# Two banded convolution layers: part of the input statistics summed by ScalarE instead of VectorE

## The chip, the cores and the metric

The kernel runs on one core of one Trainium2 chip. The metric is the device time of one execution in microseconds, the median of several runs. The core has a matrix engine (PE, with its weight loads PEld), VectorE (DVE), ScalarE (ACT), GpSimd (POOL), the queue engine SyncE (SP), and 16 DMA engines. POOL also issues DMAs of its own.

## The reference

The input `x` is 1 x 512 x 512 x 64 in float32. Two layers of one form follow each other, each adding its result to `x`. What matters here is that a layer begins with a group normalization whose 32 groups (two channels each) take mean and variance over the whole 512 x 512 picture, so that no value of a layer can be normalized before all of its input has been read.

```python
def _gn(v, G=32, eps=1e-5):
    g = v.reshape(B_, H_, W_, G, C_ // G)
    m = jnp.mean(g, axis=(1, 2, 4), keepdims=True)
    s = jnp.var(g, axis=(1, 2, 4), keepdims=True)
    return ((g - m) / jnp.sqrt(s + eps)).reshape(v.shape)
x = x + _L0_conv_ref(_gn(x), ...)   # layer norm, gated projections, band product, layer norm, projection
x = x + _L1_conv_ref(_gn(x), ...)
```

## The kernel before

The kernel has three stages. The first (`input_stats`, line 414) reads all of `x` once for the statistics of the first group normalization. The other two (`layer`, run as the generators `one` and `two`) are software pipelines over units of eight columns, with an order written out by hand in the tables `FIRST` and `SECOND`. The statistics of the second normalization are gathered inside the first layer by PE, so only the first stage concerns us.

In the first stage `x` is cut into 16 tiles `gn_x` of 128 partitions x 128 pixels x 64 channels, 4 MB each, in three buffers. SP issues one DMA per tile. For each tile DVE runs 32 `bn_stats`, one per group, each over 128 x 256 numbers, which leave mean and squared deviation of even and odd elements in `gn_st`. Then `gather` (line 432), one to five small POOL instructions (on DVE for the last tile), folds the tile's results into the running sums `gn_s1`, `gn_s2` and `gn_own`. From the third tile on, `meanwhile` lets DVE and PE do one step of `solve_layer` (line 314), the preparation of the two layers' weights. After the last tile DVE and PE reduce the sums over partitions and `group_affine` computes the scale `ga` and the shift `gb`; the first layer's first instruction `z<-z,ga` needs them.

The weights, biases and masks of both layers are fetched by small DMAs which POOL issues (`fetch_layer`, line 281, called at line 1177 before `input_stats`). Most instructions are issued through `en`, whose wrapper `InOrder` pins each of them behind the instruction traced before it on the same engine:

```python
def __getattr__(self, name):                       # class InOrder, line 483
    f = getattr(self.engine, name)
    return lambda *a, **k: tc.keep_in_program_order(f(*a, **k))   # line 491
got = [fetch_layer(i, v, tmp) for i, v in enumerate(layers)]      # line 1177; then input_stats
```

So the profile gives line 491 for most instructions, and they are told apart by their tiles. The first POOL instructions through `en` are the two memsets of `gn_s1` and `gn_s2`. After the stage SP goes on with the loads `z` of the first layer's first units, the zero fill of `left_of` and the load `on<-left_w`, which stand in its queue behind the sixteenth `gn_x`.

Of the kernel before, what the change touches and what calls it, by code (L numbers as in the profile page):

```python
# [10 lines left out]
F32 = mybir.dt.float32  # L11
I32 = mybir.dt.int32
BF16 = mybir.dt.bfloat16
AF = mybir.ActivationFunctionType
# [5 lines left out]
P = 128  # L20
# [8 lines left out]
LAG = 2 * NU  # L29
NZ = 12  # L30
NX = 6
RING = LAG + 2
WIDE = 512
NB = 32
# [97 lines left out]
def last(v: bass.AP, n: int) -> bass.AP:  # L132

    p, c = v.shape
    return v.unsqueeze(2).broadcast_to([p, c, n])
# [22 lines left out]
def tile_two_banded_layers(  # L158
# [10 lines left out]
    G = D // 2  # L169
# [45 lines left out]
    def any_bank():  # L215
        return two_banks(next(turns))[:, :512]
# [175 lines left out]
    def spread(o: bass.AP, v: bass.AP):  # L392

        nc.vector.tensor_copy(o.rearrange("p (g t) -> p g t", t=2), last(v, 2))
# [12 lines left out]
    def group_affine(mean: bass.AP, var: bass.AP, pool):  # L407

        ve = pool.tile([P, D], F32, name="g_ve")
        nc.vector.tensor_scalar(ve, var, GN_EPS, None, ALU.add)  # L410
        rsqrt(ga, ve, pool)
        nc.vector.scalar_tensor_tensor(gb, mean, -1.0, ga, ALU.mult, ALU.mult)

    def input_stats(meanwhile, afterwards):
        flat = x.rearrange("h w c -> (h w) c").rearrange("(p n) c -> p n c", p=P)
        per = L * L // P
        nt = min(128, per)
        n_t = per // nt
        with tc.tile_pool(name="gnx", bufs=3) as gx, tc.tile_pool(name="gns", bufs=1) as gs:
            st = gs.tile([P, G, n_t, 6], F32, name="gn_st")  # L420
            parts = st.rearrange("p g t (s k) -> p g (t s) k", k=3)
            add, sub, mult = ALU.add, ALU.subtract, ALU.mult

            def two(nm: str):
                return gs.tile([P, G, 2], F32, name=nm)

            own, s1, s2 = two("gn_own"), two("gn_s1"), two("gn_s2")
            ref = parts[:, :, 0:2, 1]
            en.gpsimd.memset(s1, 0.0)
            en.gpsimd.memset(s2, 0.0)  # L430

            def gather(t: int, engine):
                if t == 0:
                    engine.tensor_copy(own, parts[:, :, 0:2, 2])
                    return
                off = two(f"gn_off{t % 2}")
                engine.tensor_tensor(off, parts[:, :, 2 * t : 2 * t + 2, 1], ref, sub)
                engine.tensor_tensor(s1, s1, off, add)
                engine.tensor_tensor(off, off, off, mult)
                engine.tensor_tensor(s2, s2, off, add)  # L440
                engine.tensor_tensor(own, own, parts[:, :, 2 * t : 2 * t + 2, 2], add)

            for t in range(n_t):
                xt = gx.tile([P, nt, D], F32, name="gn_x")
                en.sync.dma_start(xt, flat[:, t * nt : (t + 1) * nt, :])
                for g in range(G):
                    en.vector.bn_stats(st[:, g, t, :], xt[:, :, 2 * g : 2 * g + 2])
                gather(t, en.gpsimd if t < n_t - 1 else en.vector)
                meanwhile(t)
            afterwards()  # L450

            mean, var = two("gn_mean"), two("gn_var")
            nc.vector.scalar_tensor_tensor(mean, s1, 1.0 / n_t, ref, mult, add)
            pm = any_bank()[:, :D]
            flat2 = lambda v: v.rearrange("p g s -> p (g s)")
            nc.tensor.matmul(pm, lhsT=all_ones, rhs=flat2(mean), start=True, stop=True)
            nc.vector.tensor_tensor(var, s1, s1, mult)
            nc.vector.scalar_tensor_tensor(var, var, -1.0 / n_t, s2, mult, add)
            nc.vector.scalar_tensor_tensor(var, own, 1.0 / nt, var, mult, add)
            tot = gs.tile([P, G], F32, name="gn_total")  # L460
            nc.vector.tensor_reduce(tot, pm.rearrange("p (g s) -> p g s", s=2), AX.X, add)
            nc.vector.tensor_scalar(tot, tot, 0.5 / P, None, mult)
            nc.vector.tensor_tensor(mean, mean, last(tot, 2), sub)
            nc.vector.tensor_tensor(mean, mean, mean, mult)
            nc.vector.scalar_tensor_tensor(var, var, 1.0 / n_t, mean, mult, add)
            pv = any_bank()[:, :D]
            nc.tensor.matmul(pv, lhsT=all_ones, rhs=flat2(var), start=True, stop=True)
            mc = gs.tile([P, D], F32, name="gn_mc")
            vc = gs.tile([P, D], F32, name="gn_vc")
            spread(mc, tot)  # L470
            vg = gs.tile([P, G], F32, name="gn_vg")
            nc.vector.tensor_reduce(vg, pv.rearrange("p (g s) -> p g s", s=2), AX.X, add)
            nc.vector.tensor_scalar(
                vc.rearrange("p (g t) -> p g t", t=2), last(vg, 2), 0.5 / P, None, mult
            )
            group_affine(mc, vc, gs)
# [105 lines left out]
    def kept(u: Unit):  # L582
        en.scalar.activation(
            ZT[:, u.at % RING].rearrange("c k (n p) -> c n k p", n=2),
            u.pt.rearrange("c n (k p) -> c n k p", p=S), AF.Identity, bias=1.0,
# [10 lines left out]
    def left_kept(u: Unit):  # L596
        pt = one_bank().rearrange("c (k p) -> c k p", p=P)
        for k in range(JU // 2):
            en.tensor.transpose(
                pt[:, k], u.z[:, 2 * k : 2 * k + 2, :].rearrange("p j c -> p (j c)"), ident  # L600
            )
        u.t = ZT[:, u.at % RING]
        en.scalar.activation(u.t, pt, AF.Identity, bias=1.0)
# [5 lines left out]
    def crossed(u: Unit, q: int, w: bass.AP, b: str):  # L609

        u.banks[q], pr = take(b)
        pr = pr.rearrange("p (e k h) -> p e k h", e=2, k=JQ // 2)
        turns = ZT[:, u.at % RING], u.t
        for k in range(JQ // 2):
# [210 lines left out]
    def gates(o: Out, w: dict, b: str):  # L825
# [3 lines left out]
        for e in range(2):  # L829
            part = slice(e * D, (e + 1) * D)  # L830
            en.tensor.matmul(
                o.pg[:, e], lhsT=w["gate"][part],
                rhs=ZT[part, o.at % RING].rearrange("c k (n p) -> c (k n) p", n=2)[:, :, m.lo : m.hi],
                start=True, stop=True,
# [31 lines left out]
    def fetch(src: bass.AP, o: Out, n: int, stats: bool):  # L866
        o.xr = XR[n % NX]
        if stats:
            o.f = o.xr[:, :, 1 : 1 + 2 * D]
        else:  # L870
            o.f = o.xr.rearrange("p k c -> p (k c)")[:, : JU * D].rearrange("p (k c) -> p k c", c=2 * D)
        for e in range(2):
            en.sync.dma_start(o.f[e * S : e * S + o.blk.m], rows_of(src, o, e))
# [41 lines left out]
    def layer(src: bass.AP, dst: bass.AP, w: dict, stats: bool, then=None):  # L915
# [15 lines left out]
        if stats:  # L931
            for n in range(2):
                posts.setdefault(n - 1, []).append(lambda n=n: clear_zh(ZH[n]))
            for n in range(NX):
                posts.setdefault(n, []).append(lambda n=n: clear_xr(XR[n]))
# [235 lines left out]
    with tc.tile_pool(name="setup", bufs=1) as tmp:  # L1171
# [5 lines left out]
        got = [fetch_layer(i, v, tmp) for i, v in enumerate(layers)]  # L1177
# [20 lines left out]
        def meanwhile(t: int):  # L1198

            if t > 1:  # L1200
                next(solving, None)
# [8 lines left out]
        def afterwards():  # L1210
            for _ in solving:
                pass
            next(one)
            for z in left_of.rearrange("a (p m w) -> a p m w", p=P, w=WIDE):
                en.sync.dma_start(z, mid(nothing, z.shape[1]))

        input_stats(meanwhile, afterwards)


# [5 lines left out]
    A = keep.tile([P, H // HA, HA // 2, S, 2], F32, name="A")  # L1225
    ZT = keep.tile([P, RING, JU // 2, P], F32, name="ZT")

# [3 lines left out]

    XR = [keep.tile([P, JU // 2, 2 * D + 2], F32, name=f"XR{i}") for i in range(NX)]
    ZH = [keep.tile([H, 2, JU, S], F32, name=f"ZH{i}") for i in range(2)]

    def clear_xr(t: bass.AP):
        en.vector.memset(t, 0.0)
        for at in (0, 2 * D + 1):
            en.vector.memset(t[:, :, at : at + 1], 1.0)

    def clear_zh(t: bass.AP):  # L1240
        en.scalar.copy(t.rearrange("h n x p -> h (n x p)"), mid(nothing, 2 * JU * S // WIDE))
# [47 lines left out]
```

## Time and profile before

| what | us |
|---|---|
| median of 3 runs | 4260.02 |
| lowest and highest run | 4246.09 and 4260.52 |
| span of the profiled execution | 4279.5 |
| first stage in it, from the start to the first `z<-z,ga` | 212.5 |

The profile gives the profiled execution no time of its own beside its span, which is 19.5 us above the median. A span is read in microseconds from its start. Busy time is the time in which an engine executes; register, semaphore and DMA-issuing instructions don't count as busy. In a timeline each row has a start, a length, the engine, the line, the operation with its tiles, how many instructions were merged into it, and in brackets how long the engine idled before it and what released it. Rows of one engine may overlap a little.

### The profile page before, as it was taken

To read this page: it belongs to the slowest core of one execution; us is meant where nothing else is said; L and a number is where in the kernel's file an instruction comes from. 1 tells how busy PE (TensorE), PEld (TensorE's weight loads), DVE (VectorE), ACT (ScalarE), POOL (GpSimd) and SP (SyncE) were. 2 spreads that over 40 slices of the span, in tenths; PEclk is the share of its full clock that TensorE was granted. 3 is DMA by queue.
4 is the path that set the end of the run, shared out by engine and by line. 5 is a ranking of instruction groups with operands and counts; after the bars stand their busy time and mean duration, and the time that the engine had idled before them with its cause. 6 is when DMAs were issued, how large, how long until landed. Compare 5 with 4: busy or idle time off the path is not lost.

```text
span 4279.5 us, 223070 instructions
## 1 busy us (share of the span) xinstructions
PE 3741.4 (87%) x94986; PEld 3208.3 (75%) x94986; DVE 3681.0 (86%) x9911; ACT 3320.3 (78%) x6372; POOL 3584.7 (84%) x4566
## 2 busy tenths in 40 slices
PE   0158999999999999999975889999999898989998
PEld 0057888888888888888864778787878787878786
DVE  8968888888888888888867889898989898989897
ACT  0047888888888888888863778888889788978887
POOL 2368999999999999999837789898989898989883
PEclk9989999999999999999997999999999999999999
DMA  9843545454545454545344354545454545444533
GB/s 396 321 102 96 150 112 152 117 147 114 152 115 151 116 152 117 153 115 155 104 119 114 98 141 120 145 120 148 121 147 119 146 116 145 123 142 122 149 105 96
DMA packets 695718, 596.25 MB, mean 139 GB/s; under 512 B 138310, under 2 KB 549990, under 8 KB 692420
## 3 DMA queue, kind: packets, MB, share of 16 engines
q1 hardware_dynamic: 692212, 580.43, 47.6%
q8 instruction: 748, 12.26, 1.2%
q14 instruction: 246, 2.02, 0.2%
q0 software_dynamic: 2512, 1.56, 0.1%
HBM read 436.71 MB, written 149.74 MB: 137 GB/s over the span
## 4 chain that ended last, share of the span: by engine, by line
PE 77%; issue 4%; POOL 3%; DVE 3%; SPq 2%; DMA 2%; ACT 2%; POOLq 0%; DVEq 0%; ACTq 0%
PE banks L491 59%; PE bank L491 14%; PE acc L491 4%; POOL z L491 3%; SPq L491 2%; DMA z<-mid_x 1%; POOL on L491 1%; DVE ZH L491 1%; DVE sto L491 1%; DVE RO L491 1%; ACT RO L491 0%; DVE z L491 0%; ACT on L491 0%; DVE XR L491 0%; ACT sg L491 0%
## 5 line engine op out<-in xcount | busy, mean ns | idle before, releaser
L491 ACT ACTIVATE on<-RO,nm,rs 128x128 f32<-128x128 f32 x2484 | 1144.3, 499 | 176.0 <-PE banks L491 150.4
L491 POOL TENSOR_SCALAR on<-RO,rs,nm 128x128 f32<-128x128 f32 x2124 | 958.6, 463 | 354.7 <-PE banks L491 308.4
L491 PE MATMUL banks<-pack,ZT 64*128 64x128 f32 x9216 | 1000.4, 287 | 28.5 <-DVE RO L491 13.9
L491 PE MATMUL banks<-pack,zT 64*128 64x128 f32 x9216 | 947.0, 277 | 3.7 <-issue 3.7
L491 DVE TENSOR_TENSOR RO<-banks,sg 128x512 f32<-128x512 f32 x1152 | 778.3, 684 | 181.9 <-ACT sg L491 158.6
L491 PEld LDWEIGHTS banks<-pack,ZT 64*128 64x128 f32 x9216 | 765.2, 191 | 152.9 <-ACT zT L491 35.6
L491 DVE BATCH_NORM_STATS2 sto<-RO 128x6 f32<-128x256 f32 x2304 | 852.5, 412 | 3.0 <-ACT RO L491 3.0
L491 DVE SCALAR_TENSOR_TENSOR ZH<-banks,pack,ZH 128x896 f32<-128x896 f32 (+1 forms) x576 | 667.4, 1159 | 198.2 <-PE banks L491 153.4
L491 ACT ACTIVATE sg<-banks 128x512 f32<-128x512 f32 x1170 | 691.6, 595 | 171.7 <-PE banks L491 133.0
L491 POOL TENSOR_TENSOR z<-z,ga 128x512 f32<-128x512 f32 x556 | 719.2, 1294 | 111.3 <-DMA z<-mid_x 91.0
L491 PE MATMUL banks<-RO,A 64*64 64x64 f32 x36864 | 699.4, 223 | 122.7 <-issue 117.5
L491 PEld LDWEIGHTS banks<-RO,A 64*64 64x64 f32 x36864 | 623.3, 136 | 222.8 <-issue 160.3
L491 PEld LDWEIGHTS banks<-pack,zT 64*128 64x128 f32 x9216 | 747.9, 192 | 5.0 <-issue 4.1
L491 POOL TENSOR_TENSOR z<-z,gb 128x512 f32<-128x512 f32 x556 | 717.8, 1291 | 3.5
L491 PE MATMUL bank<-pack,ZH 128*64 128x64 f32 x18432 | 666.3, 226 | 21.1 <-DVE ZH L491 11.2
L491 PEld LDWEIGHTS bank<-pack,ZH 128*64 128x64 f32 x18432 | 593.2, 139 | 111.3 <-issue 56.0
L491 ACT COPY RO<-banks 128x1024 f32<-128x1024 f32 x540 | 542.8, 1011 | 163.3 <-PE banks L491 154.1
L491 POOL TENSOR_TENSOR z<-z,rs 128x512 f32<-128x512 f32 x586 | 617.2, 1060 | 50.7 <-DVE rs L491 48.7
L491 POOL TENSOR_TENSOR z<-z,sti 128x512 f32<-128x512 f32 x586 | 621.9, 1071 | 35.8 <-DVE sti L491 31.8
L491 ACT ACTIVATE ZH<-banks 128x896 f32<-128x896 f32 (+1 forms) x576 | 535.4, 929 | 83.1 <-PE bank L491 55.4
L491 PE MATMUL banks<-ZT,pack 64*128 64x448 f32 (+1 forms) x2304 | 573.3, 572 | 2.6 <-DVE ZH L491 1.4
L491 DVE BATCH_NORM_STATS2 sti<-z 128x6 f32<-128x128 f32 x2344 | 509.4, 282 | 63.8 <-POOL z L491 62.9
(202 smaller groups left out, 4053.8 us busy)
## 6 DMA issues: line engine op xcount, KB each, us to landing
z<-in_x_dram SPq DMA_DIRECT2D x576, 128.0 KB
A<-left_of SPq DMA_DIRECT2D x576, 128.0 KB
z<-mid_x SPq DMA_DIRECT2D x576, 128.0 KB
gn_x<-in_x_dram SPq DMA_DIRECT2D x16, 4096.0 KB
XR<-in_x_dram SPq DMA_DIRECT2D x448, 112.0 KB
mid_x<-XR SPq DMA_DIRECT2D x448, 112.0 KB
XR<-mid_x SPq DMA_DIRECT2D x448, 112.0 KB
out_dram<-XR SPq DMA_DIRECT2D x448, 112.0 KB
```

The lines of the kernel that those rows point to most:

```text
L491: return lambda *a, **k: tc.keep_in_program_order(f(*a, **k))
```

## The change

For all tiles but the first, VectorE handles only the groups 0 to 22. The other nine (`GA = 9`, `cut = 23`) are handled by `by_sums`: for each group ScalarE runs two activations over the same 128 x 256 numbers, Identity and Square, each with a bias read from `gn_back` and each summing its output into one number per partition (`accum_out`, tile `gn_got`). The outputs themselves go to a scratch tile `gn_aside`, of which there are two, one for even and one for odd tiles; all 18 activations of a tile write the same one. Six POOL instructions then turn the 18 sums into the form in which `bn_stats` leaves mean and squared deviation, and write it to `gn_st`. The bias `gn_back` is minus the mean of the first tile, one POOL instruction behind the first tile's `bn_stats`.

```diff
--- before.py
+++ after.py
@@ -29,6 +29,7 @@
 LAG = 2 * NU
 NZ = 12
 NX = 6
+GA = 9
 RING = LAG + 2
 WIDE = 512
 NB = 32
@@ -426,6 +427,8 @@
 
             own, s1, s2 = two("gn_own"), two("gn_s1"), two("gn_s2")
             ref = parts[:, :, 0:2, 1]
+            cut = G - GA
+            back = gs.tile([P, GA], F32, name="gn_back")
             en.gpsimd.memset(s1, 0.0)
             en.gpsimd.memset(s2, 0.0)
 
@@ -440,11 +443,36 @@
                 engine.tensor_tensor(s2, s2, off, add)
                 engine.tensor_tensor(own, own, parts[:, :, 2 * t : 2 * t + 2, 2], add)
 
+            def by_sums(t: int, xt: bass.AP):
+
+                aside = gs.tile([P, nt, 2], F32, tag=f"gn_aside{t % 2}", name="gn_aside")
+                got = gs.tile([P, 2, GA], F32, tag=f"gn_got{t % 3}", name="gn_got")
+                for g in range(GA):
+                    c = slice(2 * (cut + g), 2 * (cut + g) + 2)
+                    for n, f in enumerate((AF.Identity, AF.Square)):
+                        en.scalar.activation(
+                            aside, xt[:, :, c], f, bias=back[:, g : g + 1],
+                            accum_out=got[:, n, g : g + 1],
+                        )
+                off, sq = got[:, 0], got[:, 1]
+                side = gs.tile([P, 2, GA], F32, tag=f"gn_side{t % 2}", name="gn_side")
+                en.gpsimd.tensor_scalar(side[:, 0], off, 0.5 / nt, None, mult)
+                en.gpsimd.tensor_tensor(side[:, 1], side[:, 0], off, mult)
+                en.gpsimd.tensor_tensor(side[:, 1], sq, side[:, 1], sub)
+                en.gpsimd.tensor_tensor(side[:, 0], side[:, 0], back, sub)
+                to = parts[:, cut:, 2 * t : 2 * t + 2]
+                en.gpsimd.tensor_scalar(to[:, :, :, 1], last(side[:, 0], 2), 1.0, None, mult)
+                en.gpsimd.tensor_scalar(to[:, :, :, 2], last(side[:, 1], 2), 0.5, None, mult)
+
             for t in range(n_t):
                 xt = gx.tile([P, nt, D], F32, name="gn_x")
                 en.sync.dma_start(xt, flat[:, t * nt : (t + 1) * nt, :])
-                for g in range(G):
+                for g in range(cut if t else G):
                     en.vector.bn_stats(st[:, g, t, :], xt[:, :, 2 * g : 2 * g + 2])
+                if t == 0:
+                    en.gpsimd.tensor_scalar(back, ref[:, cut:, 0], -1.0, None, mult)
+                else:
+                    by_sums(t, xt)
                 gather(t, en.gpsimd if t < n_t - 1 else en.vector)
                 meanwhile(t)
             afterwards()
```

## Rows read from the trace of the kernel before

**Rows 1.** The page, part 1: busy time, share of the span, instructions.

```profile
span 4279.5 us, 223070 instructions
PE 3741.4 (87%) x94986; PEld 3208.3 (75%) x94986; DVE 3681.0 (86%) x9911; ACT 3320.3 (78%) x6372; POOL 3584.7 (84%) x4566
```

**Rows 2.** Busy time by window: PE, PEld, DVE, ACT, POOL, clock, DMA share, GB/s.

```profile
0.00:50.00 50.00, 0.00 (x0) 0.00 (x0) 32.86 (x106) 1.28 (x1) 14.97 (x34) 1.00 0.97 397
...
150.00:200.00 50.00, 3.88 (x8) 1.92 (x8) 48.89 (x163) 0.00 (x0) 9.59 (x25) 1.00 0.90 318
```

**Rows 3.** Timeline of VectorE in the first stage.

```profile
14.12 20.97 DVE L491 BATCH_NORM_STATS2 gn_st<-gn_x 128x6 f32<-128x256 f32 x64 [10.87 <-DMA gn_x<-in_x_dram]
35.61 10.54 DVE L491 BATCH_NORM_STATS2 gn_st<-gn_x 128x6 f32<-128x256 f32 x32 [0.52 <-DMA gn_x<-in_x_dram]
...
193.96 10.53 DVE L491 BATCH_NORM_STATS2 gn_st<-gn_x 128x6 f32<-128x256 f32 x32
204.59 0.27 DVE L491 TENSOR_TENSOR gn_off<-gn_st 128x64 f32<-128x64 f32 x1
...
212.52 1.72 DVE L491 TENSOR_TENSOR z<-z,ga 128x512 f32<-128x512 f32 x1
```

**Rows 4.** Timeline of SP's DMA issues in the first stage.

```profile
0.74 165.65 SPq L491 DMA_DIRECT2D gn_x<-in_x_dram  x16
166.44 26.21 SPq L491 DMA_DIRECT2D z<-in_x_dram  x30
```

**Rows 5.** Timeline of POOL from the start to its first statistics.

```profile
8.66 0.52 POOL L294 DMA_DIRECT2D raw<-in_L_conv_Wrg_dram  x1 [2.57 <-DMA raw<-in_L_conv_Wr_dram]
...
45.85 0.58 POOL L305 DMA_DIRECT2D mq<-in_L_conv_src_mask_dram  x1 [1.04 <-DMA brow<-in_L_conv_bl_dram]
...
47.97 0.55 POOL L294 DMA_DIRECT2D raw<-in_L_conv_Wr_dram  x1 [1.41 <-DMA brow<-in_L_conv_blg_dram]
...
122.22 0.50 POOL L311 DMA_DIRECT2D ci<-in_L_conv_src_mask_dram  x1 [2.42 <-DMA ci<-in_L_conv_src_mask_dram]
122.71 0.25 POOL L491 MEMSET gn_s<- 128x64 f32 x2
122.89 0.30 POOL L491 COPY gn_own<-gn_st 128x64 f32<-128x64 f32 x1
```

**Rows 6.** DMA issues up to 220 us: count, KB each, median us to landing.

```profile
spare<-later_pack POOLq DMA_DIRECT2D x1, 498.5 KB, 4.0
...
brow<-in_L_conv_br_dram POOLq DMA_DIRECT2D x2, 0.5 KB, 18.2
```

**Rows 7.** ScalarE's groups by shape, whole span: busy us, mean ns, idle before.

```profile
L491 ACT ACTIVATE on<-RO,nm,rs 128x128 f32<-128x128 f32 x2484 | 1144.3, 499 | 176.0 <-PE banks L491 150.4 <-POOL on L491 19.4 <-POOL z L491 3.0
L491 ACT ACTIVATE sg<-banks 128x512 f32<-128x512 f32 x1170 | 691.6, 595 | 171.7 <-PE banks L491 133.0 <-DVE RO L491 9.4 <-DVE A L491 2.3
L491 ACT COPY RO<-banks 128x1024 f32<-128x1024 f32 x540 | 542.8, 1011 | 163.3 <-PE banks L491 154.1
...
L491 ACT COPY acc<-sto 128x32 f32<-128x32 f32 x72 | 13.9, 192 | 2.0 <-DVE sto L491 2.0
```

**Rows 8.** Timeline of VectorE, two memsets that write one tile.

```profile
1.17 0.17 DVE L1174 MEMSET half<- 128x128 f32 x1
1.41 0.28 DVE L1176 MEMSET half<- 64x64 f32 x2
```

**Rows 9.** Timeline of ScalarE inside the first layer.

```profile
386.22 0.20 ACT L491 COPY acc<-sto 128x32 f32<-128x32 f32 x1
386.45 0.22 ACT L491 ACTIVATE acc<-sto 128x32 f32<-128x32 f32 x1
386.60 0.58 ACT L491 ACTIVATE ZT<-banks 128x512 f32<-128x512 f32 x1
387.08 0.59 ACT L491 ACTIVATE zT<-banks 128x512 f32<-128x512 f32 x1
```

**Rows 10.** POOL's groups by shape, 0 to 215 us: busy us, mean ns, idle before.

```profile
L491 POOL TENSOR_TENSOR gn_s<-gn_s,gn_off 128x64 f32<-128x64 f32 x28 | 9.0, 320 | 2.1
```

## The prediction

> **What bounds the kernel now.** I first read the page's busy times [rows 1]: VectorE, ScalarE and POOL are all busy for about four fifths of the span, so no engine total decides, and the change has to be judged in the one stage that it touches. That stage runs from 0 to 212.5 us, where the first `z<-z,ga` waits for the statistics [rows 3]; it is 5% of the span. The windows [rows 2] show three things there. ScalarE does nothing but one table load. VectorE is near full from about 14 us on (48.89 of 50 us late in the stage). And the DMA engines were at 0.97 with 397 GB/s at the start. A 4 MB tile (4.194 million bytes) at 397 GB/s takes 10.56 us, and its 32 `bn_stats` take 10.53 us [rows 3]: DMA and VectorE are level. VectorE falls behind only by the weight preparation between the tiles and by the 14.1 us before the first tile has landed. The timeline of VectorE shows tile after tile to 204.5 us, then 7.9 us of small instructions to `ga` (204.59 to 212.52). SP's sixteenth `gn_x` goes out at about 166 us, when VectorE has released a buffer [rows 4].
>
> The view that decides the case is POOL's own timeline [rows 5]. POOL issues the small weight DMAs and may start each only when one issued eight earlier has landed (8.66 us: 2.57 us idle until `raw` had landed); with the `gn_x` stream beside them such a DMA lands after some 18 us [rows 6]. So POOL is still issuing at 122.22 us. The two memsets of `gn_s1` and `gn_s2` need no input at all, yet they run at 122.71, right behind the last of these DMAs: they are pinned behind them. Before the change nothing waits for POOL, which catches up on its small sums from 122.9 us on.
>
> **The change part by part.** *Removed:* nine of 32 `bn_stats` in 15 tiles, 135 of them. At 10.53/32 = 0.329 us each that is 44.4 us of VectorE [rows 3]. Were nothing else added, VectorE would need 7.6 us for a tile plus some 0.6 for preparation, below the DMA's 10.56, so the DMA would set the pace.
>
> *Added wait, and when ScalarE starts.* Every activation of `by_sums` reads `gn_back`. That is a POOL instruction issued through the same wrapper, behind the two memsets, hence behind all weight DMAs [rows 5]. Its data is there at 24.6 us; its turn in the queue is not. What is queued behind it: ScalarE has nothing else, but a tile's buffer is released only when ScalarE has read it. Tile 0 needs no ScalarE, so tile 3 still loads, landing at about 14.1 + 3 x 10.7 = 46 us (10.7 is the step between the first and the third tile). Then three buffers hold tiles 1 to 3, SP's `gn_x` 4 waits, and the stream stops. From here on POOL's DMAs have the DMA engines for themselves. At 46.4 us 44 issues are left before the memsets (47.97 to 122.22 us), 23.7 us of issue time by their rows. Do they still wait for landings? Away from the full stream, 498.5 KB landed in 4.0 us [rows 6], and eight issues of 0.54 us cover 4.3 us, so hardly. I add 2 us for what is in flight at 46 us and 0.7 for memsets and `gn_back`: 46.4 + 23.7 + 2.7 = 72.8, and ScalarE starts at **73 us**. Bounds: 69 without waits and with a few issues earlier, 123 as before if nothing gets faster. I take the value near the lower end because the stream that made the landings slow is certainly absent.
>
> That step leans on one DMA delaying another. The Trainium skill's opening page "Trainium Kernel Development and Optimization" (Key Constraints) says that DMAs issued from SP, ACT and POOL run on the same 16 DMA engines and interleave; the 18 us landing beside the full stream agrees with it [rows 6]. If the queues were separate instead, POOL would be no earlier than 123 us, which is the third rival below.
>
> *One accumulating pass.* The trace has none, so it is built from neighbours [rows 7]. A 128x512 pass without a bias from memory takes 595 ns, a 128x1024 copy 1011 ns: 0.81 ns per element, so 256 elements take 387 ns. A 128x128 `on`, with a scale and a bias from memory, takes 499 ns where the same line gives 283: 108 ns for each such operand. With one bias: 495 ns. Normally successive passes overlap by 0.10 us (`ZT` at 386.60 for 0.58 us, the next at 387.08 [rows 9]). Here all 18 write the same `gn_aside`, and the trace shows what a second write to one tile does: the second memset of `half` starts 0.07 us after the first ended [rows 8] where neighbours overlap, and ScalarE's two writes to `acc`, 386.22 for 0.20 us then 386.45, have a gap of 0.03 us. So I take 495 + 30 = 525 ns without overlap. The sum must also be read out to `gn_got`; no row shows that. It costs between nothing and a smallest copy with its gap, 0.22 us [rows 7, 9]. It moves one number per partition, so I take under half, 0.085. One pass: **0.61 us**; bounds 0.39 (overlap, free readout) and 0.75. A tile is then 18 x 0.61 = 11.0 us, 15 tiles 165 us.
>
> The Trainium skill's page "ScalarE: Activation LUTs" (What ACT_TABLE_LOAD costs) gives a pass with one such operand as about 280 ns + 0.833 ns per element, 493 ns here, and says that back-to-back passes overlap by about 93 ns. Its duration agrees with the 495 worked out from the rows; its overlap would make the pass 0.40 us and belongs to the first rival.
>
> *Sum of the stage.* ScalarE at 11.0 us per tile is slower than the DMA at 10.56, and once started has three tiles ready, so it never waits: 73 + 165 = 238 us. Check: `gn_x` 4 goes out at 84 us and lands by 98, ScalarE wants it at 106. VectorE at 8.2 us per tile is ahead, and POOL with six and five instructions of some 0.35 us has 4 us of work per tile. All that is covered by ScalarE. Behind the last tile come six dependent POOL instructions, 320 ns and a gap of 0.06 each by the nearest row [rows 10], 2.3 us, and a hand-over of 0.1, which used to be hidden because VectorE finished alone. Then the same 7.9 us to `ga`. The first `z<-z,ga` comes at 238 + 2.4 + 7.9 = 248.3 instead of 212.5: **+36 us**. SP's later loads move too: its last `gn_x` goes out when tile 12 is read, at 73 + 132 = 205 us, 43 us ahead of `ga` where it was 46 [rows 3, 4], so the `z` loads stay hidden. If that cover were gone, their 26 us of issue would be the price. The first layer needs `ga`, so the shift passes on whole, and its work is unchanged. No second table load is charged; one would be 1.28 us [rows 2]. The sum in the profile: 4279.5 + 36 = 4315; against the median of the runs, 19.5 us lower, 4260 + 36 = **4296 us**.
>
> **The rivals.** *DMA sets the pace after the late start.* If a pass costs under 0.55 us, ScalarE is the faster one and waits. Then `gn_x` 4 goes out at 73 + 18c (c the pass), is in use 13.4 us later as tile 0 was, tile 15 follows 11 x 10.56 us behind, and ScalarE ends 18c after that: 202.6 + 36c in all, which passes 73 + 270c at c = 0.554. With c = 0.525 that is 221.5 and with c = 0.39 it is 216.6, plus 10.3 to `ga`: +19 and +14 us, 4279 and 4274. Against it stands the shared scratch tile.
>
> *ScalarE starts in time, faster.* If `gn_back` were put ahead of the weight DMAs, ScalarE would start at about 25 us, end at 190 and `ga` would come at 200: -12 us, 4248; with c = 0.5 the DMA would set the pace and end by some 183, -19 us, 4241. The point at which it decides is a start at 37 us with c = 0.61. The memsets at 122.71 speak against it: they had every freedom and stayed behind the DMAs.
>
> *POOL isn't relieved.* If the weight DMAs keep their pace, ScalarE starts at 123 us, and everything comes 50 us later still: +86 us, 4346. Half of the relief gives 98 us and +61, 4321. For it: each of POOL's DMAs has many small pieces, and no row shows them alone.
>
> **How the numbers follow.** About 0.5%, 21 us, is what a measurement of this kernel can tell from no change. My forecast has 0.58, with its own range of 4285 to 4315 (a pass of 0.57 to 0.68). The DMA-paced rival has 0.20, the unrelieved POOL 0.15, the start in time 0.07. The range has to reach the DMA-paced end, less a few us for an earlier start and the runs' spread, and half way into the unrelieved one: 4272 to 4330. Faster by over 0.5% needs an early start and cheap passes together, and a little more than they give: 0.03. Within 0.5% are the other early starts and the DMA-paced cases, which end at +14 to +20 us, less those where POOL is also a little late: 0.22. Slower has the rest, 0.75.
>
> **What would show it.** ScalarE's first pass near 73 us, right behind a POOL instruction `gn_back` that follows the last `ci` DMA; a stop in SP's `gn_x` issues between about 25 and 84 us and a hole in the DMA rate; POOL's issues in close order after 46 us; passes 0.61 us apart without idle time between tiles; VectorE idle in the middle of the stage, waiting for `gn_x`; `z<-z,ga` near 248 us. The prediction is wrong if `gn_back` runs early, if ScalarE's passes come in under 0.5 us, or if the first layer takes up part of the shift.

## The result and the profile after

The changed kernel takes 4298.35 us (median of 5 runs, 4290.62 to 4302.86), the kernel before 4259.38 (median of 5, 4246.09 to 4260.52): a ratio of 1.0091 [1.0075, 1.0106]. That is 39.0 us slower, where +36 was predicted. The profiled execution after has a span of 4292.3 us and took 4294.12.

The page, part 1, of the kernel after (it answers to [rows 1]):

```profile
span 4292.3 us, 223599 instructions
PE 3740.1 (87%) x94986; PEld 3205.7 (75%) x94986; DVE 3636.3 (85%) x9776; ACT 3479.1 (81%) x6912; POOL 3596.4 (84%) x4657
```

The totals did what the change says, and tell nothing of the time: VectorE fell by 44.7 us (3681.0 to 3636.3), ScalarE rose by 158.8 (3320.3 to 3479.1). The windows of the kernel after (start and end, length, then PE, PEld, DVE, ACT, POOL, clock, DMA share, GB/s; they answer to [rows 2]) show where it went:

```profile
25.00:50.00 25.00, 2.47 (x5) 1.64 (x6) 18.56 (x57) 1.28 (x1) 7.96 (x15) 1.00 0.81 322
50.00:75.00 25.00, 1.91 (x4) 0.53 (x3) 5.45 (x17) 3.27 (x11) 22.30 (x47) 1.00 0.10 15
75.00:100.00 25.00, 0.00 (x0) 0.00 (x0) 4.66 (x15) 23.77 (x81) 5.76 (x22) 1.00 0.61 244
100.00:150.00 50.00, 6.98 (x14) 3.43 (x14) 39.08 (x129) 47.58 (x160) 12.18 (x45) 1.00 0.93 379
```

From 50 to 75 us the DMA engines are at 0.10 with 15 GB/s, VectorE has 5.45 us of work and ScalarE 3.27; only POOL is full (22.30 of 25). From 75 us on ScalarE is the full one. The timeline of POOL (start, duration, operation, and in brackets the idle time before it with what ended it; it answers to [rows 5]):

```profile
46.44 0.56 POOL L306 DMA_DIRECT2D mq<-in_L_conv_src_mask_dram  x1 [0.95 <-DMA brow<-in_L_conv_bl_dram]
...
47.05 1.03 POOL L295 DMA_DIRECT2D raw<-in_L_conv_Wr_dram  x1
...
70.52 0.51 POOL L312 DMA_DIRECT2D ci<-in_L_conv_src_mask_dram  x1
71.02 0.25 POOL L519 MEMSET gn_s<- 128x64 f32 x2
71.22 0.31 POOL L519 TENSOR_SCALAR gn_back<-gn_st 128x9 f32<-128x9 f32 x1
...
240.60 0.25 POOL L519 TENSOR_SCALAR gn_side<-gn_got 128x9 f32<-128x9 f32 x1 [6.29 <-ACT gn_aside L519]
...
241.75 0.49 POOL L519 TENSOR_SCALAR gn_st<-gn_side 128x18 f32<-128x18 f32 x2
```

`gn_back` stands behind the last `ci` DMA, which came 51.7 us earlier than before (70.52 against 122.22), because the stream had stopped (experiments 1 and 4 show that it is the stream): from 47.05 to 71.02 us POOL issued its 44 DMAs nearly without a pause. How fast those land is in the DMA issues of the kernel after, 46 to 71 us (count, KB each, median us to landing; they answer to [rows 6]):

```profile
raw<-in_L_conv_Wr_dram POOLq DMA_DIRECT2D x2, 32.0 KB, 2.2
...
brow<-in_L_conv_br_dram POOLq DMA_DIRECT2D x1, 0.5 KB, 2.1
```

`brow` took 18.2 us beside the stream [rows 6] and 2.1 without it. The Trainium skill's page "DMA: Bandwidth & Descriptors" (Anatomy of one DMA — SWDGE (gpsimd) path) fits about 2.0 us plus the bytes at 436 GB/s for one such DMA; the rows of the stopped stream agree with it, the 18.2 us of the running one do not.

ScalarE's timeline in the kernel after: its only table load in the stage, the first passes, a tile boundary, the last readout.

```profile
25.08 1.28 ACT L519 ACT_TABLE_LOAD   x1 [25.08 <-DMA gn_x<-in_x_dram]
71.57 0.51 ACT L519 ACTIVATE gn_aside<-gn_x,gn_back 128x256 f32<-128x256 f32 x1 [45.21 <-POOL gn_back L519]
71.99 0.19 ACT L519 ACTIVATION_READ_ACCUMULATOR gn_aside<-gn_x,gn_back 128x1 f32 x1
72.21 0.51 ACT L519 ACTIVATE gn_aside<-gn_x,gn_back 128x256 f32<-128x256 f32 x1
...
82.77 0.18 ACT L519 ACTIVATION_READ_ACCUMULATOR gn_aside<-gn_x,gn_back 128x1 f32 x1
82.86 0.49 ACT L519 ACTIVATE gn_aside<-gn_x,gn_back 128x256 f32<-128x256 f32 x1
...
240.97 0.19 ACT L519 ACTIVATION_READ_ACCUMULATOR gn_aside<-gn_x,gn_back 128x1 f32 x1
```

ScalarE waits 45.21 us for `gn_back` and then for nothing: the 15 tiles run from 71.57 to 241.16 without a bracket, 11.29 us for the first (82.86 - 71.57), 0.628 per pass on average (169.59 / 270). The readout of the sum (`ACTIVATION_READ_ACCUMULATOR`) is an instruction with a row of its own, a thing no row of before could show. Of VectorE's timeline in the kernel after (it answers to [rows 3]):

```profile
47.87 7.58 DVE L519 BATCH_NORM_STATS2 gn_st<-gn_x 128x6 f32<-128x256 f32 x23
95.34 7.60 DVE L519 BATCH_NORM_STATS2 gn_st<-gn_x 128x6 f32<-128x256 f32 x23 [39.89 <-DMA gn_x<-in_x_dram]
...
106.74 7.60 DVE L519 BATCH_NORM_STATS2 gn_st<-gn_x 128x6 f32<-128x256 f32 x23 [2.96 <-DMA gn_x<-in_x_dram]
...
242.06 0.27 DVE L519 TENSOR_TENSOR gn_off<-gn_st 128x64 f32<-128x64 f32 x1 [14.06 <-POOL gn_st L519]
...
249.92 1.71 DVE L519 TENSOR_TENSOR z<-z,ga 128x512 f32<-128x512 f32 x1
```

VectorE idles 39.89 us for the fifth `gn_x` and 14.06 for POOL at the end. The first `z<-z,ga` comes at 249.92 instead of 212.52: +37.4 us, against +39.0 of the medians. SP's timeline in the kernel after (it answers to [rows 4]) has the last `gn_x` at 207.6 and the `z` loads issued by 234.2, 15.8 us ahead of `z<-z,ga`, so those stay hidden:

```profile
0.72 206.87 SPq L519 DMA_DIRECT2D gn_x<-in_x_dram  x16
207.65 26.50 SPq L519 DMA_DIRECT2D z<-in_x_dram  x30
```

Two spans can't be subtracted here. Behind `z<-z,ga` the profile of before takes 4279.5 - 212.5 = 4067.0 us and that of after 4292.3 - 249.9 = 4042.4. The nine profiles below take 4044 to 4073 for the same work, in no order with the edits. Part of that goes with the chip: 4047 to 4058 us in experiments 1 to 4 (one chip, median of before 4270.2 us), 4057 to 4073 in 5 to 8 (a second, 4277.7), 4044 in 9 (a third, 4261.4). So the first stage is judged by where `z<-z,ga` stands, and the whole kernel by medians.

### The profile page after: what moved, and what is told of

Read it like the earlier page. It is cut to its first block, busy times and chain, and to the rows that moved or that the text cites. A ratio compares the mean times of both kernels' runs of the same rounds, so it can differ in the third digit from the quotient of the medians.

```text
span 4292.3 us, 223599 instructions
## 1 busy us (share of the span) xinstructions
PE 3740.1 (87%) x94986; PEld 3205.7 (75%) x94986; DVE 3636.3 (85%) x9776; ACT 3479.1 (81%) x6912; POOL 3596.4 (84%) x4657
## 4 chain that ended last, share of the span: by engine, by line
PE 77%; issue 4%; DVE 4%; POOL 2%; ACT 2%; SPq 2%; DMA 2%; POOLq 0%; DVEq 0%; ACTq 0%
PE banks L519 59%; PE bank L519 14%; PE acc L519 4%; POOL z L519 2%; SPq L519 2%; DMA z<-mid_x 1%; DVE RO L519 1%; DVE sto L519 1%; DVE ZH L519 1%; POOL on L519 1%; ACT on L519 0%; ACT sg L519 0%; DVE XR L519 0%; DVE z L519 0%; ACT RO L519 0%
## 5 line engine op out<-in xcount | busy, mean ns | idle before, releaser
L519 POOL TENSOR_SCALAR on<-RO,rs,nm 128x128 f32<-128x128 f32 x2124 | 948.9, 458 | 344.7 <-PE banks L519 295.8
L519 PE MATMUL banks<-pack,ZT 64*128 64x128 f32 x9216 | 1000.9, 288 | 25.4 <-DVE RO L519 11.5
```

## The experiments

Each median is compared with that of the kernel before on the same chip, whose own median lay between 4259.4 and 4277.7 us in these comparisons. All times of `z<-z,ga` in one table, with the distance to before's 212.5:

| kernel | z<-z,ga at | moved | median less before's | ratio |
|---|---|---|---|---|
| the change | 249.9 | +37.4 | +39.0 | 1.0091 [1.0075, 1.0106] |
| 1 `gn_back` on VectorE | 241.3 | +28.8 | +28.7 | 1.0067 [1.0045, 1.0089] |
| 2 two scratch tiles | 222.6 | +10.1 | +8.9 | 1.0017 [1.0003, 1.0031] |
| 3 `gn_back` on VectorE, a `gn_got` per tile | 205.0 | -7.5 | -8.4 | 0.9979 [0.9966, 0.9992] |
| 4 (3) and two scratch tiles | 201.5 | -11.0 | -14.5 | 0.9968 [0.9954, 0.9982] |
| 5 five groups | 222.5 | +10.0 | +10.3 | 1.0030 [1.0014, 1.0045] |
| 6 one group | 232.8 | +20.3 | +13.8 | 1.0049 [1.0027, 1.0070] |
| 7 (4), weights of layer two later | 211.1 | -1.4 | -2.1 | 1.0001 [0.9987, 1.0015] |
| 8 (7), sums settled in batches | 199.5 | -13.0 | -14.7 | 0.9972 [0.9959, 0.9985] |
| 9 (8), no POOL arithmetic | 193.2 | -19.3 | -17.4 | 0.9964 [0.9948, 0.9980] |

In all rows but that of experiment 6 the two differences lie within 4 us of each other; there the interval (+11.5 to +29.9 us, from 1.0027 and 1.0070 of 4277.7) holds the 20.3. Within these intervals the shift of the first stage passes through to the end whole, in either direction. Medians of experiments on different chips can't be compared directly, only their ratios.

**1. `gn_back` on VectorE.** Is it the place in POOL's queue that makes ScalarE late?

```
-                    en.gpsimd.tensor_scalar(back, ref[:, cut:, 0], -1.0, None, mult)
+                    en.vector.tensor_scalar(back, ref[:, cut:, 0], -1.0, None, mult)
```

> The bias gn_back is computed by VectorE instead of POOL; everything else as in the changed kernel. Theory (POOL's queue holds ScalarE up): ScalarE's first pass moves from 71.6 to about 25 us, but only three tiles get through. The sums gn_got have three slots, POOL reads them, and POOL is still at its weight DMAs, so ScalarE stops before tile 4 until POOL is through with them. The stream of gn_x then stops three tiles later than in the changed kernel (about 79 us), and POOL gets its turn at about 93. ScalarE ends near 231, the first z<-z,ga comes at about 240 us instead of 249.9, the time is about 4288. Rival (only the start of the first pass matters): no stop, end of ScalarE near 195, z<-z,ga at 204, about 4251.

ScalarE's timeline in this run, its first pass and the one that waits:

```profile
27.26 0.51 ACT L519 ACTIVATE gn_aside<-gn_x,gn_back 128x256 f32<-128x256 f32 x1
...
96.86 0.51 ACT L519 ACTIVATE gn_aside<-gn_x,gn_back 128x256 f32<-128x256 f32 x1 [35.61 <-POOL gn_side L519]
```

And POOL's, where its arithmetic begins:

```profile
95.00 0.25 POOL L519 MEMSET gn_s<- 128x64 f32 x2
...
95.44 0.32 POOL L519 TENSOR_SCALAR gn_side<-gn_got 128x9 f32<-128x9 f32 x1
```

The first pass comes at 27.26 instead of 71.57, so the place of `gn_back` in the queue is what held it. Yet only 8.6 us of the shift go away. After three tiles ScalarE has filled the three `gn_got` buffers, and POOL, which must read them first, does so at 95.44, behind the same weight DMAs. The same queue stops the same stream again, three tiles later, and POOL's arithmetic begins 24 us later than in the change (95.00 against 71.02).

**2. Two scratch tiles.** Identity and Square write to different tiles; the start stays late.

```
-                aside = gs.tile([P, nt, 2], F32, tag=f"gn_aside{t % 2}", name="gn_aside")
+                asides = [
+                    gs.tile([P, nt, 2], F32, tag=f"gn_aside{n}", name="gn_aside") for n in range(2)
+                ]
...
-                            aside, xt[:, :, c], f, bias=back[:, g : g + 1],
+                            asides[n], xt[:, :, c], f, bias=back[:, g : g + 1],
```

> Identity and Square write two different scratch tiles in turn; everything else as in the changed kernel, the late start too. Theory (each pass waits for the one before it because both write one tile): passes come 0.51 us apart instead of 0.626, as at the one place of the changed kernel's trace where the scratch tile changes. A tile then takes 9.2 us, less than its DMA, the DMA sets the pace after the start at 71.6 us, and z<-z,ga comes at about 229 us instead of 249.9; time about 4277. Rival (the 0.626 us are the engine's own time for a pass and its readout): no change, z<-z,ga at 250, 4298.

ScalarE's timeline in this run:

```profile
71.46 0.51 ACT L521 ACTIVATE gn_aside<-gn_x,gn_back 128x256 f32<-128x256 f32 x1 [45.09 <-POOL gn_back L521]
71.88 0.19 ACT L521 ACTIVATION_READ_ACCUMULATOR gn_aside<-gn_x,gn_back 128x1 f32 x1
71.97 0.49 ACT L521 ACTIVATE gn_aside<-gn_x,gn_back 128x256 f32<-128x256 f32 x1
72.37 0.19 ACT L521 ACTIVATION_READ_ACCUMULATOR gn_aside<-gn_x,gn_back 128x1 f32 x1
72.46 0.49 ACT L521 ACTIVATE gn_aside<-gn_x,gn_back 128x256 f32<-128x256 f32 x1
```

The readout begins 0.42 us after the start of its pass (their rows overlap by 0.09), as in the kernel after. But the next pass now begins 0.09 after the readout's start instead of 0.22: a pass is 0.49 us instead of 0.63. The shared output tile cost 0.14 us per pass, and the same 0.49 us row stands in the kernel after at its tile boundary (82.86), where the scratch changes. The Trainium skill's page "ScalarE: Activation LUTs" (What ACT_TABLE_LOAD costs) says that back-to-back passes overlap by about 93 ns. The rows show that much between a pass and its readout (0.09), and without a shared output between a readout and the next pass (0.10).

ScalarE is now faster than the DMA, the first rival's case. Its time came out 8 us shorter than that rival's formula gives with a pass of 0.49 (202.6 + 36 x 0.49 + 10.3 = 230.5): start, landing, pace and the way from the last sum to `ga` were each a little long in it (the tiles come 10.37 us apart, not 10.56). The 229 expected was 6 us too late as well. VectorE's timeline in this run, tile 4 and the end:

```profile
92.62 7.61 DVE L521 BATCH_NORM_STATS2 gn_st<-gn_x 128x6 f32<-128x256 f32 x23 [37.59 <-DMA gn_x<-in_x_dram]
...
222.61 1.72 DVE L521 TENSOR_TENSOR z<-z,ga 128x512 f32<-128x512 f32 x1
```

So with passes that don't pace, the late start alone is worth +10 us; the slow pass adds the other 27. The two prices don't stand alone: without the late start the slow pass costs only 3.5 us (experiments 3 and 4, 205.0 and 201.5), because in 4 another wait takes over.

**3. No wait for POOL's queue.** `gn_back` on VectorE as in 1, and a buffer of `gn_got` for each tile; the scratch tile is shared again.

```
-                got = gs.tile([P, 2, GA], F32, tag=f"gn_got{t % 3}", name="gn_got")
+                got = gs.tile([P, 2, GA], F32, tag=f"gn_got{t}", name="gn_got")
```

> gn_back on VectorE and a slot of its own in gn_got for each tile, so that ScalarE waits for POOL nowhere; the shared scratch tile stays. Theory: ScalarE starts at 25 us and sets the pace with 11.27 us per tile, ends near 195, z<-z,ga at about 205 us, 8 us ahead of the kernel before: about 4251. POOL is not relieved, reaches the sums at about 120 us and catches up. Rival (the summing on POOL becomes the end of the stage): POOL is at tile 15 only after 200 us, and z<-z,ga comes after 215, 4262 or more.

VectorE's timeline in this run:

```profile
121.88 0.48 DVE L519 TENSOR_SCALAR brow<-brow 1x640 f32<-1x640 f32 x1 [12.13 <-DMA brow<-in_L_conv_bog_dram]
...
205.03 1.72 DVE L519 TENSOR_TENSOR z<-z,ga 128x512 f32<-128x512 f32 x1
```

205.0 against an expected 205: the stream no longer stops for POOL, and the kernel is 8 us faster than before the change. The arithmetic is the same, the passes as slow as in the change (the scratch tile is still shared), and only two things no longer wait for POOL's queue. So that queue, and what followed from it, was worth 44.9 us (249.9 to 205.0), more than the whole +39. A new wait shows: VectorE stands 12.13 us for a bias row of the second layer's weights, one of POOL's DMAs that is slow beside the running stream.

**4. The same with two scratch tiles** (the edits of 2 and 3 together).

> As the run with gn_back on VectorE and a slot per tile, and the two scratch tiles as well. Theory: passes 0.51 us apart from 25 us on, 9.2 us per tile, under the 10.6 us of the DMA, so the DMA sets the pace from end to end: tile 15 lands at about 175, ScalarE ends at 184, z<-z,ga at about 194 us, 18 us ahead of the kernel before: about 4241. Rival (the stream of gn_x is slowed by more readers, or POOL ends it): z<-z,ga between 200 and 212, 4247 to 4259.

VectorE's timeline in this run:

```profile
130.37 0.48 DVE L521 TENSOR_SCALAR brow<-brow 1x640 f32<-1x640 f32 x1 [21.19 <-DMA mi<-in_L_conv_src_mask_dram]
...
201.49 1.72 DVE L521 TENSOR_TENSOR z<-z,ga 128x512 f32<-128x512 f32 x1
```

The expected 194 was missed by 7 us; 201.5 lies in the rival's range, though neither more readers nor POOL's sums are the reason. VectorE arrives at the weight preparation when it did in 3 (130.37 - 21.19 = 109.18 us, there 121.88 - 12.13 = 109.75) and stands 21.19 us instead of 12.13, because the DMAs that it needs land later: the last `brow` 16.3 us after its issue, where it took 9.1 in 3. In 3 the stream thinned out from 115 to 125 us (shares of 0.91 and 0.84 in two windows of 5 us), while here it stays full up to 125 us (1.02 and 1.00): the faster ScalarE holds no tile back. That this is why they land later fits these windows, but no run varies it alone. While VectorE stands, its tiles' buffers aren't released, and then the stream does stop; this run's windows:

```profile
115.00:120.00 5.00, 0.00 (x0) 0.00 (x0) 0.00 (x0) 3.89 (x16) 1.13 (x2) 1.00 1.02 423
...
125.00:150.00 25.00, 7.34 (x14) 3.68 (x14) 19.49 (x59) 13.27 (x54) 19.25 (x59) 1.00 0.55 214
```

The first of these rows also settles what makes POOL's DMAs slow. In the change VectorE stood still while the stream did, so either could have been the cause. Here VectorE stands (0.00 us) while the stream runs (423 GB/s), and the five `brow` issued from 104 to 114 us still land only after 16.3 to 18.6 us. In experiment 1 it is the other way round: from 78 us on the stream has stopped (a DMA share of 0.11 to 95 us), VectorE works on a tile until 85.8, and the `raw` and `brow` issued then land after 1.7 to 2.2 us. So it is the stream and not VectorE. ScalarE is ruled out by the kernel before, where it does next to nothing (1.28 us in the first 50 [rows 2]) and they are as slow.

**5 and 6. Fewer groups for ScalarE**, all else as in the change: `GA = 5` and `GA = 1` for `GA = 9`. One group leaves nearly no work to ScalarE, but its pass still needs `gn_back`.

> The changed kernel with five groups on ScalarE instead of nine (GA = 5); the late start stays. Theory (a start at 71.6 us, and from there the slowest of ScalarE, DMA and VectorE): ScalarE needs 10 x 0.626 = 6.3 us per tile, VectorE 27 x 0.329 = 8.9 and some 1.25 for preparation, the DMA 10.4, so the DMA sets the pace behind the stop: tile 4 in use at 90, tile 15 at 204, done at 213, z<-z,ga at about 221 us, 9 us later than the kernel before: about +0.2%. Rival (the loss goes with the work on ScalarE): 5/9 of 37, z<-z,ga at 233.

> The changed kernel with one group on ScalarE (GA = 1); the late start stays. Theory: ScalarE's work is next to nothing (1.25 us per tile), so this is the price of the stop alone. VectorE, with 10.2 us of statistics and 1.25 of preparation per tile, sets the pace again after tile 4 comes into use at 85 us: 12 tiles end at 223, z<-z,ga at about 231 us, 18 us later than the kernel before, more than with five groups. Rival (the loss goes with the work on ScalarE): 1/9 of 37, z<-z,ga at 217.

VectorE's timeline with five groups, tile 4 and the end:

```profile
90.58 8.90 DVE L519 BATCH_NORM_STATS2 gn_st<-gn_x 128x6 f32<-128x256 f32 x27 [33.71 <-DMA gn_x<-in_x_dram]
...
222.54 1.72 DVE L519 TENSOR_TENSOR z<-z,ga 128x512 f32<-128x512 f32 x1
```

And with one group:

```profile
85.56 10.21 DVE L519 BATCH_NORM_STATS2 gn_st<-gn_x 128x6 f32<-128x256 f32 x31 [27.41 <-DMA gn_x<-in_x_dram]
...
232.76 1.72 DVE L519 TENSOR_TENSOR z<-z,ga 128x512 f32<-128x512 f32 x1
```

Nearly no work moved, and still +20 us: this is the price of the wait alone, while VectorE's 10.21 us per tile and the preparation pace what follows. Five groups give +10, nine +37. The order isn't by the work moved, because the pace after the stop is VectorE's at one group and ScalarE's at nine. At five VectorE and the DMA are level: the DMA share is 1.00 with 423 GB/s from 90.5 to 200 us, and VectorE is busy for 121.9 of the 124.0 us to the end of its statistics and waits for no tile. The expected times (221 and 231) came within 2 us, but at five groups the expectation had the DMA alone set the pace, and it is VectorE that ends last.

**7. The second layer's weight preparation three tiles later**, on top of 4, so that VectorE meets it when the DMAs have landed.

```
-            if t > 1:
+            for _ in range(0 if t < 2 or 8 <= t <= 10 else 2 if t in (13, 14) else 1):
                 next(solving, None)
```

> As the run with gn_back on VectorE, a slot per tile and two scratch tiles, and the weight preparation of the second layer three tiles later, because there VectorE waited 21 us for weights that POOL had not yet fetched. Theory one (the rest of the gain was lost in that wait): no stop of gn_x any more, z<-z,ga at about 194 us instead of 201.5, about 0.2% less time. Theory two (POOL takes over as the limit): without the stop its weight DMAs last until about 141 us, then it has 15 tiles of 3.4 us to fold, until 192, and z<-z,ga comes at about 201 us, no gain.

POOL's timeline in this run:

```profile
149.99 0.25 POOL L521 MEMSET gn_s<- 128x64 f32 x2
```

VectorE's:

```profile
201.10 0.27 DVE L521 TENSOR_TENSOR gn_off<-gn_st 128x64 f32<-128x64 f32 x1 [21.68 <-POOL gn_st L521]
...
211.13 1.71 DVE L521 TENSOR_TENSOR z<-z,ga 128x512 f32<-128x512 f32 x1
```

It came out slower than 4, and later than either theory said. VectorE no longer stands for weights, so the stream never stops and POOL's DMAs stay slow to the end: its arithmetic begins at 149.99 instead of 136.50. It then has 15 tiles of small sums to catch up on, and VectorE waits 21.68 us for them, though ScalarE's last sum was out by 180.1. The place of the limit was as theory two had it, its time 10 us too early.

**8. POOL settles ScalarE's sums four tiles at a time**, on top of 7. The core of it:

```
+                t0 = {4: 1, 8: 5, 12: 9, 13: 13, 14: 14, 15: 15}.get(t)
+                if t0 is not None:
+                    settle(t0, t + 1)
+                    for u in range(t0, t + 1):
+                        gather(u, en.gpsimd if u < n_t - 1 else en.vector)
```

> As the run with the later preparation, and POOL turns ScalarE's sums into statistics for four tiles at a time (tiles 1 to 4, 5 to 8, 9 to 12, then singly), six instructions for four tiles instead of 24. Theory two: POOL has about 37 us to do behind its weight DMAs instead of 51 and is through by 180, before ScalarE ends at 184, so only now z<-z,ga comes at about 194 us, 18 us ahead of the kernel before, -0.4%. Theory one: the same 194 us as the run before it.

VectorE's timeline in this run:

```profile
189.46 0.27 DVE L533 TENSOR_TENSOR gn_off<-gn_st 128x64 f32<-128x64 f32 x1 [9.38 <-POOL gn_st L533]
...
199.50 1.71 DVE L533 TENSOR_TENSOR z<-z,ga 128x512 f32<-128x512 f32 x1
```

11.6 us are won, and VectorE's wait for POOL falls from 21.68 to 9.38 us. So POOL's catching up was the limit, and it still is in part: the 194 expected was missed by 5.5 us. The folding tile by tile is still with POOL.

**9. No POOL arithmetic in the stage**: VectorE settles and folds in three batches (tiles 0 to 8, 9 to 11, 12 to 15), on top of 8.

```
+                if t in (9, 12, n_t - 1):
+                    t0, t1 = {9: (0, 9), 12: (9, 12)}.get(t, (12, n_t))
+                    settle(max(t0, 1), t1)
+                    fold(t0, t1)
```

> As the run with batches, but settling and folding are done by VectorE in three batches (tiles 0 to 8, 9 to 11, 12 to 15), with no POOL arithmetic in the stage at all. Theory (behind the weight DMAs POOL was the last to end): the DMA sets the pace to the end, ScalarE is done with tile 15 at about 181 us, then 1.5 us to settle and 2.7 to fold four tiles, and z<-z,ga comes at about 192 us, 20 us ahead of the kernel before and 7 ahead of the batched run: about -0.45%. Rival (the batches hold VectorE up, which already shares its time with the weight preparation): gn_x stops near tiles 9 to 13, z<-z,ga at 200 or later, no gain over the batched run.

The windows of this run:

```profile
0.00:50.00 50.00, 0.00 (x0) 0.00 (x0) 27.19 (x89) 23.49 (x90) 14.90 (x34) 1.00 0.98 395
...
71.00:84.00 13.00, 1.81 (x6) 1.43 (x6) 12.82 (x41) 11.72 (x48) 3.19 (x6) 1.00 1.02 435
84.00:150.00 66.00, 6.44 (x10) 2.68 (x10) 57.55 (x182) 55.26 (x223) 15.64 (x29) 1.00 1.00 410
```

And VectorE's timeline at the end of the stage:

```profile
180.69 0.15 DVE L530 TENSOR_SCALAR gn_side<-gn_got 128x36 f32<-128x36 f32 x1
...
193.20 1.72 DVE L530 TENSOR_TENSOR z<-z,ga 128x512 f32<-128x512 f32 x1
```

The DMA engines are full from the start to 150 us, 395 to 435 GB/s, and VectorE and ScalarE end within a us of each other (ScalarE's last sum at 179.96, VectorE's settling at 180.69). The median is 4244.05 us, 17.4 below before (ratio 0.9964 [0.9948, 0.9980]). It has the earliest `z<-z,ga` of all kernels here; its ratio can't be told from those of 4 and 8, whose intervals overlap with it. The tiles now come at the DMA's pace, and behind the last of them stand 12.5 us of small instructions on VectorE and PE (180.69 to 193.20).

## Why the prediction held

Its terms against what they measured, for the first `z<-z,ga`:

| term | predicted | measured |
|---|---|---|
| ScalarE starts | 73 | 71.57 |
| 270 passes | 165 (0.61 each) | 169.6 (0.628 each) |
| hand-over through POOL | 2.4 | 0.9 (241.16 to 242.06) |
| to `z<-z,ga` | 7.9 | 7.86 |
| sum | 248.3 | 249.9 |

**The start.** Shown, not only argued: experiment 1 takes `gn_back` out of POOL's queue and the start moves to 27.26. It is also steady: the four profiles with the late start (the change, 2, 5 and 6) have the memsets at 70.91 to 71.03. The 44 issues took 24.0 us (47.05 to 71.02), 23.7 were read from the rows. The 2 us for transfers in flight weren't needed: from 47.05 us on there is one pause of 0.21 us, and the landings of about 2 us lie inside the 4 us of eight issues.

**The pass.** The sum was near, its parts were not. I had 525 ns for the pass and 85 for the readout. In the rows the pass lasts 510, the readout 186, they overlap by 0.09, and the next pass begins 0.03 after the readout's end. The wait for the shared scratch tile follows the readout, not the pass. Its size, 0.14 us per pass, is shown by experiment 2. The 85 ns for the readout were a choice between bounds without a row; net it adds 0.12 us, and a pass 15 ns shorter than forecast makes up for part of that. That the sum came within 3% is in part luck, and so is the whole: the passes are 4.6 us longer than forecast, the start and the hand-over 2.9 us shorter. At the predicted 0.61 and at the measured 0.63 ScalarE paces, so nothing tipped over; at 0.49 it would have, and the time would have been the first rival's.

**The pace and the cover.** ScalarE ran 15 tiles without a wait, VectorE waited for `gn_x` in the middle, and SP's `z` loads stayed ahead of `ga`, all as said. The hole in the DMA is the stop that was predicted. VectorE's preparation was put too low, at 0.6 us per tile: between 14.12 and 204.59 us before, 22 us are left beside the statistics, some 5 of them waits, so 1.2 us for each of 14 steps. Nothing hung on it, since 7.6 + 1.2 us is still below ScalarE's 11. The hand-over was shorter because two of POOL's six instructions on the last tile ran on the Identity sums before the last Square was read out, and 9 elements take 0.20 us where I had read 0.32 from a 64-wide row.

**The whole time.** The sum against the profile, a span of 4315, was 23 us off the span of after (4292.3), the one against the median 2.4 us off (4296 against 4298.35). The row of before was from an execution whose later layers took some 25 us longer than those of after. Correcting to the median was the right step; why one execution's layers take longer than another's on one chip stays open.

**The rivals.** POOL was relieved, so the third didn't come. The second, a start in time, was priced wrong: experiment 1 builds it, and instead of 200 us it gives 241.3. The rival left out that the three `gn_got` buffers also wait for POOL's queue; only with that wait gone too (experiment 3) does `z<-z,ga` come near, at 205.0, the passes being 0.628 instead of 0.61 and the start 26.6 instead of 25. POOL's relief has a reverse side that the prediction didn't follow to its end: it comes only because the stream stops. Each cure of a wait let the stream run on and kept POOL's DMAs slow, and the next thing behind them became the limit: `gn_got` (1), VectorE's weight preparation (4), POOL's own sums (7 and 8). Of the runs without the late start only the one in which nothing in the stage needed POOL in time (9) ended with the stream's last tile. A fourth `gn_x` buffer, which would let the stream run longer before it stops, wasn't tried.

## What to carry to other kernels

Before an operation is put on an engine, read what stands ahead of it in that engine's queue, and what waits for it: here an instruction of 0.3 us, with its data there at about 25 us, ran at 71 us and stopped a stream that filled the DMA engines. What a group moved to an idle engine brings hangs on what on its way goes through a queue that is behind: the same nine groups gave +37.4 us here, and -1.4 to -19.3 in the runs where ScalarE waited for that queue nowhere (3, 4, 7, 8 and 9). The cheap test is to move almost nothing (experiment 6) and see what the wait alone costs. And when one wait is cured, price the next one along the same queue before building on the cure.

## What the hardware showed that was not expected

- An accumulating pass of ScalarE is two instructions in the trace. The readout (186 ns) begins 0.42 us after the start of its pass, and a next pass that writes the same output tile begins only after the readout's end: 0.63 us per pass of 128x256 against 0.49 with two output tiles in turn. Whether the chip or a wait in the program holds it back, the rows don't say.
- A POOL DMA of 0.5 KB that landed in 2.1 us without the `gn_x` stream took 18.2 beside it, a factor of nine for the same bytes, and with it POOL's instructions moved by 50 us.
- The stream itself can run faster than the 397 GB/s of [rows 2]: experiment 9 holds 395 to 435 GB/s, with 410 over 66 us.
- Executions of one and the same work behind the first stage differ by up to 31 us (4042 to 4073) in their profiles. Part of it goes with the chip (4047 to 4058, 4057 to 4073 and 4044 us on three of them); no row that I read explains the rest.
